# Two chained cross-attentions over 32 batches: the heads of the first scored twice, four at once, and the order of keys and first batches rewritten

## The chip, the cores and the metric

The kernel runs on one core of a Trainium2 chip. The metric is the time of one execution on the device in microseconds (us). A core has five engines with a queue each, executed in order: TensorE (PE, with its weight loads PEld), VectorE (DVE), ScalarE (ACT), GpSimd (POOL) and SyncE (SP), which here only issues DMAs. Products land in PSUM, eight banks of 2 KB per partition; everything else is computed in SBUF.

## The reference

Inputs are `x` and `ctx`, both 32 batches of 256 tokens by 256 columns, and the weights. L0 attends from x to ctx with 16 heads of 16 columns, but adds only batch 0's result, `att[0]`, to all batches. L1 is an attention of one head per batch, an MLP of four hidden units on its result, a second attention over that, and two scaled sums. All is float32.

```python
def _L0_xattn_ref(tgt, memory, Wq, Wk, Wv):
    q = (tgt @ Wq.T).reshape(B, N, NH, dk).transpose(0, 2, 1, 3)   # k, v from memory
    scores = jnp.einsum('bhqd,bhkd->bhqk', q, k) * scale
    probs = jax.nn.softmax(scores, axis=-1)
    att = jnp.einsum('bhqk,bhkd->bhqd', probs, v)
    tgt2 = att[0]                       # batch 0 alone, tokens by 256
    return tgt + tgt2
...
    norm_X = _layernorm(input_features, norm1_w, norm1_b)          # input_features: ctx
    norm_F_L = _layernorm(query_feature, norm2_w, norm2_b)         # query_feature: x after L0
    attended = _attention(norm_F_L, norm_X, norm_X, scale)
    h = jax.nn.gelu(attended @ fc1_w.T + fc1_b, approximate=False)
    cross_attended = h @ fc2_w.T + fc2_b
    norm_cross = _layernorm(cross_attended, norm3_w, norm3_b)
    self_attended = _attention(norm_cross, norm_cross, norm_cross, scale)
    skip_connect = cross_attended + gamma1 * self_attended
    return norm_F_L + gamma2 * skip_connect
```

## The kernel before

A batch is a tile of 128 partitions by 2 by 256: two tokens to a partition. All of x stays in SBUF (`x_all`); ctx comes in groups of four batches (`cq`, four buffers). The order of the instructions on each engine is the order of the program text: nothing is rescheduled (`manual_schedule`, line 69), and an instruction that waits holds up all behind it on its engine.

**Start (lines 100 to 153, 299 to 313).** SP loads batch 0 of x and ctx, small vectors, then ctx groups and x; ACT's queue loads the three weights. PE transposes x0, Wq, c0, Wk (`turned`, L179); four copies empty PSUM.

**Heads (L0).** `project(j)` (L316) makes q and k of heads 4j to 4j+3, each head on 32 partitions of its own. `head_scores(p)` (L376) scores two heads, queries on partitions; `exp_pair` (L348) takes the row maxima on DVE (L351) and the exponentials on ACT (L356); `head_turned` (L381) transposes the weights on PE and copies them by ACT and DVE (L388, L390); `head_values` multiplies by the values, `head_weighted` (L400) divides and writes a part of `att`. `head_step(s)` (L527) runs these in a pipeline over eight pairs of heads, and a list beside each step (lines 540 to 550) places the work for L1: `stats_c(n)` (DVE, the statistics of the keys of batch n, L188), `moments_c(q)` (POOL, mean and 1/deviation of four batches: eight small operations, L198 to L210, one of them a power, L203), `norm_c(n)` (POOL, two operations in place, L255), `turn_c(n)` (PE, four transposes, and a copy to `nxT`, L275), and the setups of the small matrices.

**Between.** `att` is added to batches 0 to 7 on DVE (L638) and to the others by DMAs that accumulate (L562). Batches 0 and 1, 2 and 3, 4 to 7 get moments on POOL (`moments_x`), `norm_x(n)` (one half on POOL, L262, the other on ACT, L264) and `turn_x(n)` (transposes, then `nfT` on ACT, L572).

**The loop over batches.** `first_step(s)` (from line 682) runs for s from 0 to 34. In step s, in this order: `cross_turned(s-2)` (transposes of weights, `pt_e`), statistics of x of batch s+8 and keys of batch s+12 (DVE), at every fourth step `moments_both` (POOL: keys and queries of four batches each), `turn_x(s+1)`, `norm_x(s+4)`, `turn_c(s+4)` from s = 4 on, `norm_c(s+8)`, the products with values at some steps, and `cross_scores(s)` (L590; maximum on DVE, L598; exponentials on ACT, L601). POOL also clears tiles in steps 8 to 17 (L711). Work of the MLP and of the second attention is put between and beside later steps (`third_a` to `third_d`, on POOL and DVE; `scale_skip` on POOL from step 25 on). A last part finishes the second attention and stores the output.

The line that ties norming and turning of keys to a step is, before:

```python
        if s + QB < B and s >= QB:
            turn_c(s + QB)
        if s + 2 * QB < B:
            norm_c(s + 2 * QB)
```

Of the kernel before, what the change touches and what calls it, by code (L numbers as in the profile page):

```python
# [15 lines left out]
P = 128  # L16
D = 256
# [10 lines left out]
def tile_xattn_seq(  # L28
# [49 lines left out]
    ps0 = l0_psum.enter_context(tc.tile_pool(name="ps0", bufs=2, space=PSUM))  # L78
# [26 lines left out]
    for name, w in (("q", wq), ("k", wk_w), ("v", wv)):  # L105
        w_nat[name] = wk.tile([P, NC, D], F32, tag="e", name=f"w{name}_nat", bufs=6)
        nc.scalar.dma_start(w_nat[name], w.rearrange("(c p) d -> p c d", p=P))
# [38 lines left out]

    ident = const.tile([P, P], F32)
# [12 lines left out]
    qT = l0.tile([P, NH // 4, D], F32)  # L160
    kT = l0.tile([P, NH // 4, D], F32)
# [28 lines left out]
    def moments(st, n, name):  # L190


# [5 lines left out]
        nc.gpsimd.tensor_sub(df, st[:, :, 1:2], st[:, :, 4:5])  # L198
        nc.gpsimd.tensor_add(sm, st[:, :, 1:3], st[:, :, 4:6])
        nc.gpsimd.tensor_mul(sq, df, df)  # L200
        nc.gpsimd.tensor_scalar(v4, sm[:, :, 1:2], 4.0 / D, 4 * EPS, ALU.mult, ALU.add)
        nc.gpsimd.tensor_add(ve, v4, sq)
# [6 lines left out]
        nc.gpsimd.tensor_scalar(nm, sm[:, :, 0:1], -0.5, 0.0, ALU.mult, ALU.add)  # L209
        nc.gpsimd.tensor_mul(nmr, nm, rs)  # L210
        return rs, nmr
# [31 lines left out]

    def moments_both(q):

        rn = moments(st_of[q].rearrange("p k b t c -> p (k b t) c"), 2 * TQ, f"b{q}")
        for b in range(QB):
            mc_of[(q + 1) * QB + b] = *rn, b * NC
            mx_of[q * QB + b] = *rn, TQ + b * NC
# [21 lines left out]
    def turn_c(n, copy=nc.vector.tensor_copy):  # L271
        q, b = n // QB, n % QB
        if b == 0:
            nxT_of[q] = wk.tile([P, QB, NC, D], F32, tag="nxT", name=f"nxT_{q}", bufs=2)
        copy(nxT_of[q][:, b], turned(cq_of[q][:, b], "tp", f"c_{n}"))  # L275
# [40 lines left out]
    def project(j):  # L316
# [11 lines left out]
        nc.vector.tensor_scalar_mul(qT[:, j, :], pp[:, 0, :], DK**-0.5)  # L328
        nc.scalar.copy(kT[:, j, :], pp[:, 1, :])

    def project_values():
        nc.vector.tensor_copy(wvT, turned(w_nat["v"], "tp", "wv"))
# [10 lines left out]
        for t in range(NC):  # L343
            nc.vector.tensor_copy(
                v1[:, t, :, 0:DK], pp[:, t, :].rearrange("p (h e) -> p h e", e=DK)
            )

    def exp_pair(sc, name):  # L348

        nm = small.tile([P, 2, NC], F32, tag="nm2", name=f"nm2_{name}")  # L350
        nc.vector.tensor_reduce(nm, sc, AX.X, ALU.max, negate=True)  # L351
        es = []
        for i in range(2):
            e = wk.tile([P, NC, D], F32, tag="e", name=f"e_{name}_{i}", bufs=6)
            for qt in range(NC):
                nc.scalar.activation(  # L356
                    e[:, qt, :], sc[:, i, qt, :], AF.Exp, bias=nm[:, i, qt : qt + 1]
                )
            es.append(e)
        return es  # L360
# [15 lines left out]
    def head_scores(p):  # L376
        sc = ps0.tile([P, 2, NC, D], F32, tag="s2", name=f"sc_h{p}")
        pair_products((p, qT[:, p // 2, :], kT[:, p // 2, :], [sc[:, i] for i in range(2)]))
        e_of[p] = exp_pair(sc, f"h{p}")

    def head_turned(p):  # L381
        if p % 2 == 0:
            eT_of[p // 2] = wk.tile([P, QB, NC, D], F32, tag="eTq", name=f"eT_h{p // 2}", bufs=2)
        for i, e in enumerate(e_of.pop(p)):
            dst = eT_of[p // 2][:, p % 2 * 2 + i]
            pe = turned(e, "et", f"eh_{p}_{i}")
            if i == 0:
                nc.scalar.copy(dst, pe)  # L388
            else:
                nc.vector.tensor_copy(dst, pe)  # L390
# [4 lines left out]
    def head_values(j):  # L395
        col_of[j] = by_columns(
            tp_bank, f"h{j}", lambda kt, i: v1[:, kt, 4 * j + i, :], eT_of.pop(j)
# [59 lines left out]
    def setup_m():  # L457
# [5 lines left out]
        nc.gpsimd.tensor_scalar(m5_nmean, m5_sum, -1.0 / D, 0.0, ALU.mult, ALU.add)  # L463
        nc.gpsimd.tensor_scalar(m5c, m5, m5_nmean, 0.0, ALU.add, ALU.add)
        nc.gpsimd.tensor_mul(k6[0:NM, :], m5c, w3r)
# [49 lines left out]
    def setup_output():  # L515
        nc.gpsimd.tensor_mul(w_h, m5, g2r)
        nc.gpsimd.tensor_mul(g1r, g1r, g2r)
        nc.gpsimd.tensor_mul(tail, tail, g1r)
        nc.gpsimd.tensor_add(w_h, w_h, tail)
        nc.gpsimd.tensor_add(w_h, w_h, bias2)  # L520
        nc.gpsimd.tensor_mul(g1r, g1r, k6[0:NM, :])
# [5 lines left out]
    def head_step(s, beside=()):  # L527
        if 0 <= s - 2 < NH // 2:
            head_turned(s - 2)
        if s < NH // 2:  # L530
            head_scores(s)
        if s % 2 == 1 and 0 <= s // 2 - 1 < NH // 4:
            head_values(s // 2 - 1)
        if s % 2 == 0 and 0 <= s // 2 - 2 < NH // 4:
            head_weighted(s // 2 - 2)
        for f, *args in beside:
            f(*args)

    project(0)
    head_step(0, [(project_values,), (stats_c, 0), (stats_c, 1)])  # L540
    head_step(1, [(project, 1), (stats_c, 2), (stats_c, 3), (moments_c, 0), (setup_fc1,)])
    head_step(2, [(stats_c, 4), (setup_queries,), (norm_c, 0), (norm_c, 1)])
    head_step(3, [(project, 2), (stats_c, 5), (norm_c, 2), (norm_c, 3), (setup_m,)])
    head_step(4, [(stats_c, 6), (turn_c, 0), (setup_outer,)])
    head_step(5, [(project, 3), (stats_c, 7), (moments_c, 1), (turn_c, 1)])
    head_step(6, [(stats_c, 8), (setup_gram,), (setup_output,), (norm_c, 4), (norm_c, 5)])
    head_step(7, [(stats_c, 9), (turn_c, 2), (norm_c, 6), (norm_c, 7)])
    head_step(8, [(turn_c, 3)])
    head_step(9, [(stats_c, 10)])
    head_step(10, [])  # L550
# [34 lines left out]
    def cross_scores(n):  # L585
# [11 lines left out]
        nm = small.tile([P, NC], F32, tag="nm", name=f"nm_{n}")  # L597
        nc.vector.tensor_reduce(nm, sc, AX.X, ALU.max, negate=True)  # L598
        e = wk.tile([P, NC, D], F32, tag="e", name=f"e_{n}", bufs=6)
        for qt in range(NC):  # L600
            nc.scalar.activation(e[:, qt, :], sc[:, qt, :], AF.Exp, bias=nm[:, qt : qt + 1])  # L601
        e_of[n] = e
# [31 lines left out]
    for q in range(2, 4):  # L634
        add_attention(q * QB, (q + 1) * QB)

    def add_and_stats(n):
        nc.vector.tensor_add(x_all[:, n], x_all[:, n], att)  # L638
        stats_x(n)

    add_and_stats(0)
    add_and_stats(1)
    moments_x(0, 0, 2)
    turn_c(4, nc.scalar.copy)
    turn_c(5, nc.scalar.copy)
    values(0)
    add_and_stats(2)
    add_and_stats(3)
    turn_c(6, nc.scalar.copy)
    turn_c(7, nc.scalar.copy)  # L650
    values_turned(0)
    norm_x(0)
    norm_x(1)
    moments_x(0, 2, 4)
    values(1)
    for n in range(4, 8):
        add_and_stats(n)
    turn_x(0)
    values_turned(1)
    norm_x(2)  # L660
    norm_x(3)
    stats_c(11)
    moments_x(1, 0, 4)
    moments_c(2)
# [424 lines left out]
```

## Time and profile before

| | us |
|---|---|
| three runs | 260.51, 264.87, 264.16 (median 264.16) |
| the profiled execution | 260.04, its span 258.3 |
| mean granted clock of TensorE | 0.967 |
| kT of the first heads ready | 11.18 |
| last part of `att` ready | 52.27 |
| scores of batch 0 start; of batch 8 end | 61.71; 95.42 |

The span is the time from the first to the last instruction of that execution; 1.74 us lie around it. In a line of the timeline the first number is the start and the second the duration in us, of as many instructions as the x at its end tells; then follow the engine, the line of the code, the operation, what it writes and reads, and in brackets the idle time of the engine before it, with what ended that. A slice of the page's second part is 6.46 us.

### The profile page before, as it was taken

The page shows a single profiled execution, that of the slowest core. Times are in us where ns is not written, and L with a number is a line of the kernel's source. Part 1 is how long each engine was busy: PE and PEld are TensorE (multiplying, and loading weights), DVE is VectorE, ACT ScalarE, POOL GpSimd, SP SyncE. Part 2 cuts the span into 40 slices and gives each one's busy share as a digit, 9 for nine tenths or more (in the row PEclk, how much of TensorE's full clock was granted, in tenths as well). Part 3 has the DMA queues.
Part 4 walks back from the last instruction along what each step waited for, and adds up shares of the span by engine and source line. Part 5 has one row for each costly group of instructions (what it writes and reads, how often), then busy time and mean ns, then how long its engine had stood idle before and what let it go on. Part 6 is the DMA issues. An engine that isn't in the chain of part 4 may idle for free.

```text
span 258.3 us, 4919 instructions
## 1 busy us (share of the span) xinstructions
PE 226.9 (88%) x1797; PEld 167.3 (65%) x1797; DVE 171.8 (67%) x371; ACT 144.4 (56%) x297; POOL 185.6 (72%) x298
## 2 busy tenths in 40 slices
PE   3878989977699999999999999989999699899960
PEld 3655666645487787978888796666666356565530
DVE  1369669799738587776868565465445567877482
ACT  1126454444686787677858984656743655454610
POOL 7006827989999989999958989992419808999200
PEclk9999999997979999999999999999999979999995
DMA  6859997059398766718000000000000024343466
GB/s 204 279 190 381 384 388 278 4 100 192 63 241 221 125 202 114 213 28 141 0 3 0 0 3 0 4 0 0 0 3 0 4 81 162 123 159 132 161 237 256
DMA packets 17526, 32.76 MB, mean 127 GB/s; under 512 B 1175, under 2 KB 2142, under 8 KB 17502
## 3 DMA queue, kind: packets, MB, share of 16 engines
q1 hardware_dynamic: 12462, 23.28, 24.8%
q0 software_dynamic: 3168, 6.29, 14.7%
q10 hardware_dynamic: 1872, 2.88, 3.1%
q8 instruction: 14, 0.23, 0.4%
q14 instruction: 10, 0.08, 0.1%
HBM read 17.73 MB, written 8.39 MB: 101 GB/s over the span
## 4 chain that ended last, share of the span: by engine, by line
PE 63%; POOL 15%; DVE 12%; ACT 3%; issue 3%; DMA 1%; DVEq 0%; ACTq 0%; POOLq 0%
PE sc L590 19%; PE sc L368 9%; PE pt_x L179 5%; PE pt_c L179 4%; PE pt_e L179 4%; PE pv L282 3%; PE pu L282 3%; PE po L368 3%; POOL rs_x L203 2%; POOL r L777 2%; PE pf L282 2%; PE pp L321 2%; POOL cq L255 2%; PE ph L282 2%; DVE x_all L934 1%
## 5 line engine op out<-in xcount | busy, mean ns | idle before, releaser
L590 PE MATMUL sc<-nxT,nfT 128*128 128x256 f32 x256 | 64.3, 396 | 0.3 <-ACT nfT L572 0.3
L590 PEld LDWEIGHTS sc<-nxT,nfT 128*128 128x128 f32 x256 | 47.9, 197 | 11.5 <-issue 4.9
L598 DVE TENSOR_REDUCE nm<-sc 128x2 f32<-128x512 f32 x32 | 22.1, 691 | 37.1 <-PE sc L590 20.7
L601 ACT ACTIVATE e<-sc,nm 128x256 f32<-128x256 f32 x64 | 26.8, 470 | 26.1 <-DVE nm L598 26.1
L581 POOL TENSOR_TENSOR x_all<-x_all,w_bc 128x512 f32<-128x512 f32 x32 | 39.6, 1275 | 0.0
L572 ACT ACTIVATE nfT<-pt_x,bq,wq 128x256 f32<-128x256 f32 x64 | 33.3, 582 | 0.0
L179 PE MATMUL pt_x<-ident,x_all 128*128 128x128 f32 x132 | 21.3, 287 | 8.4 <-DMA x_all<-in_x_dram 4.3
L255 POOL TENSOR_SCALAR cq<-cq,rs_b,nmr_b 128x256 f32<-128x256 f32 x40 | 24.8, 708 | 0.0
L188 DVE BATCH_NORM_STATS2 st<-x_all 128x6 f32<-128x256 f32 x64 | 23.9, 415 | 0.3
L179 PEld LDWEIGHTS pt_x<-ident,x_all 128*128 128x128 f32 x132 | 16.2, 147 | 9.4 <-POOL wkT L153 4.2
L179 PE MATMUL pt_e<-ident,e 128*128 128x128 f32 x128 | 20.0, 276 | 2.6 <-ACT e L601 2.5
L356 ACT ACTIVATE e_h<-sc_h,nm_h 128x256 f32<-128x256 f32 x32 | 12.6, 475 | 17.1 <-DVE nm_h L351 17.1
L179 PE MATMUL pt_c<-ident,cq 128*128 128x128 f32 x132 | 20.5, 280 | 1.6 <-DVE ut L801 0.8
L275 DVE COPY nxT<-pt_c 128x512 f32<-128x512 f32 x28 | 19.0, 677 | 4.1 <-PE pt_c L179 4.1
L368 PE MATMUL po<-w_out,vt 32*128 32x256 f32 x128 | 17.9, 412 | 3.4 <-DVE vt L808 2.2
L934 DVE TENSOR_TENSOR x_all<-po,x_all 128x512 f32<-128x512 f32 x26 | 16.7, 684 | 6.0 <-PE po L368 4.2
L188 DVE BATCH_NORM_STATS2 st<-cq 128x6 f32<-128x256 f32 x56 | 20.7, 411 | 0.0
L179 PEld LDWEIGHTS pt_e<-ident,e 128*128 128x128 f32 x128 | 15.4, 141 | 7.3 <-ACT e L601 3.9
L608 ACT COPY eTq<-pt_e 128x512 f32<-128x512 f32 x32 | 18.7, 587 | 1.9 <-PE pt_e L179 1.8
L368 PE MATMUL sc<-tt,ut 32*128 32x256 f32 x128 | 19.4, 403 | 0.0
L368 PE MATMUL sc<-ut 32*128 32x256 f32 x128 | 19.4, 413 | 0.0
L179 PEld LDWEIGHTS pt_c<-ident,cq 128*128 128x128 f32 x132 | 15.5, 143 | 3.6 <-DVE ut L801 1.0
(190 smaller groups left out, 464.9 us busy)
## 6 DMA issues: line engine op xcount, KB each, us to landing
out_dram<-x_all SPq DMA_DIRECT2D x16, 512.0 KB
x_all<-in_x_dram SPq DMA_DIRECT2D x6, 1024.0 KB
x_all<-att POOLq DMA_DIRECT2D x6, 1024.0 KB, 9.2
cq<-in_ctx_dram SPq DMA_DIRECT2D x5, 1024.0 KB
cq<-in_ctx_dram ACTq DMA_DIRECT2D x2, 1024.0 KB
x_all<-in_x_dram SPq DMA_DIRECT2D x1, 1792.0 KB
cq<-in_ctx_dram SPq DMA_DIRECT2D x1, 768.0 KB
wq_nat<-in_L_xattn_Wq_dram ACTq DMA_DIRECT2D x1, 256.0 KB
```

Source lines behind the costliest of these rows:

```text
L179: nc.tensor.transpose(pt[:, dc, t * P : (t + 1) * P], src[:, t, dc * P : (dc + 1) * P], ident)
L188: nc.vector.bn_stats(st[:, t, :], src[:, t, :])
L255: nc.gpsimd.tensor_scalar(row, row, rs[:, i + t, :], nmr[:, i + t, :], ALU.mult, ALU.add)
L275: copy(nxT_of[q][:, b], turned(cq_of[q][:, b], "tp", f"c_{n}"))
L282: nc.tensor.matmul(pg[SL * b : SL * (b + 1), 0, :], weights(kc, b), moving[:, b, kc, :], start=(kc == 0), stop=(kc == NC - 1),)
L368: nc.tensor.matmul(dst[i][:, t, :], lhs[r : r + SL, t * P : (t + 1) * P], rhs[r : r + SL, :], start=True, stop=True,)
L572: nc.scalar.activation(nfT_of[n][:, dc, :], px[:, dc, :], AF.Identity, bias=bq[:, dc : dc + 1], scale=wq2[:, dc : dc + 1],)
L581: nc.gpsimd.tensor_mul(x_all[:, n], x_all[:, n], w2_bc.unsqueeze(1).to_broadcast([P, NC, D]))
L590: nc.tensor.matmul(sc[:, qt, :], nfT[:, dc, qt * P : (qt + 1) * P], nxT[:, dc, :], start=(dc == 0), stop=(dc == NC - 1),)
L598: nc.vector.tensor_reduce(nm, sc, AX.X, ALU.max, negate=True)
L601: nc.scalar.activation(e[:, qt, :], sc[:, qt, :], AF.Exp, bias=nm[:, qt : qt + 1])
L934: nc.vector.tensor_add(x_all[:, n], po[i], x_all[:, n])
```

## The change

It does the following.

- Four matmuls of zeros open PE's queue.
- Four heads are scored at once, by `pair_products` with two pairs. `head_queries(j)` scores with the queries on the partitions and takes the negative row maxima into a column of `m_all`; `head_maxima(j)` transposes these and adds them to the queries' spare row (`qmT`), against a row of ones in kT (`k_ones`); `head_keys(j)` scores again with the keys on the partitions, so that the exponentials need no maximum and no transposes. `head_turned` and `exp_pair` are gone. qT and kT have two buffers in place of four.
- `head_step(j)` runs over four foursomes, with three places for other work in each. Keys of batches 0 to 11 get statistics and moments there and just behind, `norm_c` of 0 to 9 before, 10 and 11 among the first batches; in the loop `norm_c` runs for 12 to 15 in steps 1 to 3 and, from step 8 on, for s+8. `turn_c` runs for s+7 in steps 1 to 24; `nxT` has three buffers. `load_c` of groups 4 to 7 moves.
- x of batches 0 to 3 gets `att` added, statistics, moments and norm one batch at a time, of 4 to 7 two at a time, with the small operations of the moments on DVE and only the power on POOL; batches 4 to 7 get `att` by DMA.
- The small setups of `setup_m` and `setup_output` move from POOL to DVE, several copies from DVE to ACT.

The diff, cut:

```diff
-    ps0 = l0_psum.enter_context(tc.tile_pool(name="ps0", bufs=2, space=PSUM))
+    ps0 = l0_psum.enter_context(tc.tile_pool(name="ps0", bufs=1, space=PSUM))
...
+    zeros = l0.tile([P, D], F32)
+    nc.vector.memset(zeros, 0.0)
+    idle = bank("et", "p_idle")
+    for i in range(4):
+        nc.tensor.matmul(idle[:, i % NC, :], zeros[:, 0:P], zeros, start=True, stop=True)
...
-    qT = l0.tile([P, NH // 4, D], F32)
-    kT = l0.tile([P, NH // 4, D], F32)
+    qT = l0.tile([P, 2, D], F32)
+    kT = l0.tile([P, 2, D], F32)
+    qmT = l0.tile([P, 2, D], F32)
+    m_all = l0.tile([P, 2, NC, QB, SL], F32)
+    nc.gpsimd.memset(m_all, 0.0)
...
-    def moments(st, n, name):
+    def moments(st, n, name, eng=None):
+        eng = eng or nc.gpsimd
...
-        nc.gpsimd.tensor_sub(df, st[:, :, 1:2], st[:, :, 4:5])
+        eng.tensor_sub(df, st[:, :, 1:2], st[:, :, 4:5])
...
         nc.gpsimd.tensor_tensor(
             rs.rearrange("p n o -> p (n o)"),
...
+        def product():
+            eng.tensor_scalar(nm, sm[:, :, 0:1], -0.5, 0.0, ALU.mult, ALU.add)
+            eng.tensor_mul(nmr, nm, rs)
...
-        nc.vector.tensor_scalar_mul(qT[:, j, :], pp[:, 0, :], DK**-0.5)
-        nc.scalar.copy(kT[:, j, :], pp[:, 1, :])
+        nc.vector.tensor_scalar_mul(qT[:, j % 2, :], pp[:, 0, :], DK**-0.5)
+        nc.scalar.activation(kT[:, j % 2, :], pp[:, 1, :], AF.Identity, bias=k_ones)
...
+    def head_queries(j):
+        s0, b0 = head_bank("s0", f"sq_{2 * j}")
+        odd = [bank("et", f"sq_{2 * j + 1}_{i}") for i in range(2)]
+        qk = qT[:, j % 2, :], kT[:, j % 2, :]
+        pair_products((2 * j, *qk, b0), (2 * j + 1, *qk, odd))
+        for sc, b in ((s0, slice(0, 2)), (odd[0], 2), (odd[1], 3)):
+            m = m_all[:, j % 2, :, b, DK]
+            nc.vector.tensor_reduce(
...
+    def head_maxima(j):
+        pm = bank("tp", f"pm_{j}")
+        for t in range(NC):
+            nc.tensor.transpose(
...
+        nc.vector.tensor_add(qmT[:, j % 2, :], pm[:, 0, :], qT[:, j % 2, :])
+    def head_keys(j):
+        s1, b1 = head_bank("s1", f"sk_{2 * j}")
+        s0, b0 = head_bank("s0", f"sk_{2 * j + 1}")
+        kq = kT[:, j % 2, :], qmT[:, j % 2, :]
+        pair_products((2 * j, *kq, b1), (2 * j + 1, *kq, b0))
+        eT_of[j] = wk.tile([P, QB, NC, D], F32, tag="eTq", name=f"eT_h{j}", bufs=2)
+        nc.scalar.activation(eT_of[j][:, 2:4], s0, AF.Exp)
+        nc.scalar.activation(eT_of[j][:, 0:2], s1, AF.Exp)
...
+    head_step(
+        0,
+        [(project_values,), (project, 1), (stats_c, 0)],
+        [(setup_fc1,), (stats_c, 1)],
+        [(stats_c, 2), (stats_c, 3), (moments_c, 0), (setup_queries,)],
+    )
+    head_step(
+        1,
+        [(head_values, 0), (project, 2), (norm_c, 0), (norm_c, 1)],
+        [(head_weighted, 0), (stats_c, 4)],
+        [(stats_c, 5), (stats_c, 6), (norm_c, 2), (norm_c, 3)],
+    )
+    head_step(
+        2,
+        [(head_values, 1), (project, 3), (stats_c, 7), (moments_c, 1)],
+        [(head_weighted, 1), (turn_c, 0, on_scalar), (setup_m,)],
+        [
+            (turn_c, 1, on_scalar),
+            (turn_c, 2, on_scalar),
+            *((norm_c, n) for n in range(4, 8)),
+            (stats_c, 8),
+            (setup_outer,),
+        ],
+    )
+    head_step(
+        3,
+        [(head_values, 2), (turn_c, 3, on_scalar), (load_c, 4), (stats_c, 9)],
+        [(head_weighted, 2), (stats_c, 10)],
+        [(turn_c, 4, on_scalar), (stats_c, 11), (moments_c, 2), (turn_c, 5, on_scalar)],
+    )
+    head_values(3)
+    setup_gram()
+    setup_output()
+    turn_c(6, on_scalar)
+    load_c(5)
+    norm_c(8)
+    norm_c(9)
+    stats_c(12)
+    head_weighted(3)
...
+    def add_first(n, meanwhile):
         nc.vector.tensor_add(x_all[:, n], x_all[:, n], att)
         stats_x(n)
+        ends = first_moments(n, n + 1)
+        meanwhile()
+        ends()
+    add_attention(QB, 2 * QB)
+    turn_c(7, on_scalar)
     values(0)
+    load_c(6)
+    add_first(0, lambda: stats_c(13))
     values_turned(0)
+    values(1)
     norm_x(0)
+    norm_c(10)
+    add_attention(2 * QB, 3 * QB)
+    turn_x(0)
+    add_first(1, lambda: (stats_c(14), stats_c(15)))
+    values_turned(1)
     norm_x(1)
+    norm_c(11)
+    moments_c(3)
...
-        if s + QB < B and s >= QB:
-            turn_c(s + QB)
-        if s + 2 * QB < B:
+        if 0 < s < B - 2 * QB + 1:
+            turn_c(s + 2 * QB - 1)
+        if 0 < s < QB:
+            norm_c(s + 3 * QB - 1)
+            if s == QB - 1:
+                norm_c(s + 3 * QB)
+        elif 2 * QB <= s < B - 2 * QB:
             norm_c(s + 2 * QB)
...
+            softmax = cross_scores(s)
+            if s <= QB:
+                turn_x(s + 1)
+            if s < 2:
+                add_first(s + 2, softmax)
+                norm_x(s + 2)
+            else:
+                softmax()
...
-        w = late.tile([P, TG, n, n], F32, tag=f"w{n}", name=f"w_{name}", bufs=2)
+        w = late.tile([P, TG, n, n], F32, tag=f"w{n}", name=f"w_{name}", bufs=1)
...
-        21: [(third_a, 1), (third_b, 0)],
+        21: [(third_b, 0), (third_a, 1)],
```

## The prediction

> **What bounds the kernel now.** I read first the page's busy shares and its 40 slices, for the stretches in which TensorE (PE) isn't full.
>
> ```profile
> PE 226.9 (88%) x1797; PEld 167.3 (65%) x1797; DVE 171.8 (67%) x371; ACT 144.4 (56%) x297; POOL 185.6 (72%) x298
> ...
> PE   3878989977699999999999999989999699899960
> ...
> POOL 7006827989999989999958989992419808999200
> ```
>
> PE is full from the 12th slice (71 us) to the 26th (168 us); its gaps lie before 6 us, at 52 to 71 us and at the end. GpSimd (POOL) is as full as PE from 70 to 130 us. So two engines are near the bound in the loop over batches, and a schedule that ties one closely to the other is dangerous. The chain of waits, read next, agrees: from 86 to 149 us it is PE from one end to the other, 3.75 us a step, and at 50 to 70 us it goes through POOL's moments.
>
> The third view is the timeline at step 11 of the loop. `norm_c` normalizes a batch of keys on POOL, `turn_c` transposes it on PE (`pt_c`); batch 19 is normed at step 11.
>
> ```profile
> 104.20 0.69 DVE L598 TENSOR_REDUCE nm<-sc 128x2 f32<-128x512 f32 x1 [1.43 <-ACT x_all L264]
> 104.81 0.75 DVE L188 BATCH_NORM_STATS2 st<-x_all 128x6 f32<-128x256 f32 x2
> 105.47 0.74 DVE L188 BATCH_NORM_STATS2 st<-cq 128x6 f32<-128x256 f32 x2
> ...
> 106.29 0.23 POOL L198 TENSOR_TENSOR df_b<-st 128x16 f32<-128x16 f32 x1
> ...
> 107.58 2.94 POOL L203 TENSOR_TENSOR rs_b<-ve_b,neg_half 128x16 f32<-128x16 f32 x1
> ...
> 110.99 0.56 POOL L262 TENSOR_SCALAR x_all<-x_all,rs_b,nmr_b 128x256 f32<-128x256 f32 x1
> 111.53 1.09 POOL L255 TENSOR_SCALAR cq<-cq,rs_b,nmr_b 128x256 f32<-128x256 f32 x2
> ```
>
> The scores of batch 10 ended at 104.15. DVE takes their maximum, then the statistics (to 106.2); POOL's `moments_both` takes 106.29 to 110.99, 4.70 us, of which one power is 2.94; behind it stand `norm_x`(15) and `norm_c`(19), done at 112.62: 8.47 us after the scores of batch 10. PE's step 12:
>
> ```profile
> 107.20 0.60 PE L179 MATMUL pt_e<-ident,e 128*128 128x128 f32 x4
> 107.64 0.60 PE L179 MATMUL pt_x<-ident,x_all 128*128 128x128 f32 x4
> 108.08 0.60 PE L179 MATMUL pt_c<-ident,cq 128*128 128x128 f32 x4
> 108.51 1.89 PE L590 MATMUL sc<-nxT,nfT 128*128 128x256 f32 x8
> ```
>
> At 108.08 it turns keys, then scores. Today those are batch 16, normed long ago: turning runs 4 batches ahead of scoring and norming 8.
>
> **The change, part by part.**
>
> (a) Start. Four matmuls of zeros keep PE busy before x arrives at 4.26. Today PE's first transposes take 0.213 us each (0.85 for four), later ones 0.11, though the granted clock reads 1.00. If the zeros end that slow time, the landing of the key weights (SP's queue shows it at about 6.15) sets the pace: transposes 0.45, two copies 0.8, two products 0.9, qT 0.43, kT 0.38 make kT ready at 9.35, not 11.18: **-1.8** (from 0, where PE starts slow all the same, to -2.0).
>
> (b) Heads, from kT to the last `att`: today 11.18 to 52.27, 41.1 us. The change drops 64 transposes of weights (16 times 0.44 us of PE) and 16 copies of 0.6 to 0.68 on ACT and DVE, and scores twice. Eight matmuls on four row groups take 1.1 us (202.00 to 203.13, a later stage), as four on two do today. But the maxima now stand in a chain: scores 1.1, maxima 1.23 + 0.69 + 0.69 less overlap = 2.4 (rows L351, L598), qT and sum 0.42 each, scores again 1.1, first exponential 1.03 (L924), which frees the bank for the next four heads. Walked along the queues from kT, the scores of the four foursomes start at 0, 10.6, 17.7 and 27.5: the first carries the values' products, whose bank waits for a maximum, and project 1 (to 6.95); the third carries statistics (0.7), two key copies on ACT and `setup_outer`'s transposes. The fourth scores to 28.6; maxima 31.0; statistics and sum 32.1; keys 33.2; exponentials 35.25; a key copy 35.85; values and gram 37.7; six output rows now on DVE 2.2; statistics 0.7; `att` at 41.1. **0** (from -5 to +3). The saved work is PE's and ACT's; the chain is DVE's.
>
> The Trainium skill's TensorEngine Tiling (Array Packing), section "PSUM Bottleneck", speaks against the expected gain: packing speeds the products, not the emptying of PSUM. Here 1.1 us of products face 2.4 us of maxima. By packing alone the heads would be some 7 us shorter; by that rule they aren't.
>
> (c) From `att` to the end of the scores of batch 8: today 52.27 to 95.42, 43.1 us. After: add and two statistics 1.47, five small DVE operations 1.0 (0.2 each, from rd and att), the power of two columns 0.7 (1.65 for 8, 2.92 for 16, so 0.16 a column), the product 0.35, norm 0.6, transposes 0.5, half of nfT 0.6: scores of batch 0 start 5.4 after `att`, today 9.4. Then POOL's queue: batch 1's power stands behind `norm_c`(10) 1.1 and a DMA issue 1.4 (scores at +9.8), batch 2's behind `norm_c`(11) and `moments_c`(3), 4.4 together (+15.9); batch 3's nfT stands on ACT behind the norms of 4 and 5, which wait for DVE 2.4 and a power 1.3 (+23.5); batch 4 at +28.7 (today +26.0), batch 8 ends at +44.8. **+1.7** (-5 to +4).
>
> (d) The loop. Turning now runs 7 batches ahead of scoring, norming still 8 from step 8 on: the lead falls from four steps to one. At step 12 `pt_c` turns batch 19, whose norm ends 8.47 us after the scores of batch 10, while PE arrives 3.93 after them. All that follows in PE's queue, scores 12 included, waits 4.4 us (transposes after the wait 0.35). Statistics come only after the maximum of the scores before, so POOL can't catch up: the next round is as late again. A round of four steps costs 8.8 + 1.73 + 4.23 + 4.45 = 19.2 us, not 14.94. The five places: batch 16 at step 9, 3.5 (its norm ends at 100.04 today, `pt_c` stands at 96.13); 19, 4.4, and 0.6 for 20 behind a memset and a DMA issue; 23, 4.4 (127.6 against 123.06); 27, 4.4 (142.6 against 138.05); 29 behind `third_a`, which waits for the gelu, 0.8; 31 at step 24, behind `third_c` and `moments_x` on POOL, 7.3 (today 160.64 against 153.16). **+25.4**. Below: if rows before were POOL's own backlog only, the largest lateness is paid once, 7.5; above, each place a microsecond worse, 31.
>
> (e) Clock. Where PE stood 3.3 us (56.3 to 59.7), the granted clock was 0.66 in 60 to 65 us and the scores took 2.91, not 1.99; after 2.3 us, 3.21. The five gaps of 3.5 to 7.3 us are longer: 1.0 each, **+5** (0 to +10). TensorE: Matmul & The Clock Gate, "HAM oscillation", warns of idle gaps over 3.4 us, with 3.4 us at half clock after: half of that, 1.7 a gap, would be 8.5 as an estimate.
>
> (f) End of the loop: steps 25 to 27 have no `turn_c` (three times 0.44), the waits of 0.94 (161.9) and 0.4 of the 0.78 at 169.4 go: **-2.7** (-5 to 0). The end, 200 us on, is untouched.
>
> The moments and rows moved from POOL to DVE, some 10 us, free POOL before step 8 only, where it then waits for statistics anyway; batches 4 to 7 added by one more DMA (9.2 us to landing) have 15 us until they are read. SP's queue issues the loads of keys 4 to 7 earlier, around the eight stores of `w_out` (0.66 to 0.80 each), and the first is read some 30 us later; the two issues of 0.38 that stood on ACT go. The cleared maxima (0.52, a memset of 128x512) lie before 6 us beside PE's transposes; were they late, kT is still 4 us off. Key copies moved from DVE to ACT take 0.59 for 0.68 and are counted where they stand in a chain. Fewer buffers for `e` (three live at a time) and `w` cost nothing: `third_a`(1) now stands behind its reader.
>
> Sum: -1.8 + 0 + 1.7 + 25.4 + 5 - 2.7 = **+27.6** on the profiled execution's own 260.04 us (span 258.3): **287.6**. That execution is the fastest of those shown; the median is 264.16, so the median after may lie 1 to 2% above. Below 2% a measurement of this kernel tells nothing from no change.
>
> **Rivals.** *The stalls come, the rest is kinder*: clock not lost and heads or first batches 5 to 8 us shorter, 260.04 - 1.8 - 5 + 25.4 - 2.7 = 276; for it, the heads do lose 7 us of PE work. Chance 0.28. *Only a backlog* (the other side): if POOL, freed of 10 us, holds its norms ahead, `pt_c` never waits; the loop stays at 15 us a round and the change brings 260.04 - 1.8 - 4 - 2.7 = 251 to 253. It decides at one point: `norm_c`(19) must end within 3.9 us of the scores of batch 10, not 8.5. Against it, 4.70 of moments alone are more than that. Chance 0.07. *Backlog paid once*: 260.04 - 1.8 + 7.5 - 2.7 = 263, within 2%; it needs statistics that don't wait for PE's progress, and DVE's order says they do. Chance 0.03. *Worse*: a second wait in the rounds, or cold products throughout, over 297: 0.07. The forecast, 279 to 297: 0.55. Four heads at once not running at once would add 4 us to it, no case of its own.
>
> The range leaves out 251 to 263 and the worst: **271 to 297**. Slower by over 2%: 0.90; within 0.03; faster 0.07.
>
> **What would show it.** Right: in the page's slices PE has holes at steps 9, 12, 16, 20 and 24, PE's idle before `pt_c` released by POOL cq (L255 today, some 20 us in all), POOL idle before `df_b` released by DVE statistics, rounds of 19 us between the scores of batches 10, 14 and 18. (a): kT near 9.4; (b) `att` near 50.5. Wrong: rounds of 15 us, or `pt_c` released by nothing. What would upset it most is a power shorter than 2.9 us, or statistics ahead of the maximum.

## The result, and the profile after

| | before | after |
|---|---|---|
| runs, us | 260.51, 264.87, 264.16, 263.94 (median 264.05) | 295.98, 296.07, 296.15, 297.75 (median 296.11) |
| profiled execution; its span | 260.04; 258.3 | 295.98; 293.8 |
| mean granted clock | 0.967 | 0.910 |

The changed kernel takes 1.128 times as long (95% interval 1.116 to 1.140). The forecast was 287.6 us with 271 to 297. Executions of one kernel differ with the granted clock, mostly by some 5 us (the kernel before from 259 to 265 us in all, `lead6` below 269.5 and 274.3 to 274.6) and once by 17 (`l4_both`), and a profile shows one of them (`lead4`, `filled`, `l4_project` and `l4_rows` the longest, `lead6` the shortest), so terms are read from stretches of the profiles and not from times alone. The two profiles of the table, cut at the places that the forecast's terms use (kT ready, last part of `att`, end of the scores of batch 8, start of those of batch 24, end; the loop from start to start of the scores), account for all 35.5 us of the spans, to a tenth:

| stretch | before | after | difference | forecast |
|---|---|---|---|---|
| to kT | 11.18 | 9.71 | -1.5 | -1.8 (a) |
| kT to `att` | 41.1 | 46.9 | +5.8 | 0 (b) |
| `att` to the end of scores 8 | 43.2 | 44.9 | +1.7 | +1.7 (c) |
| scores 8 to scores 24 | 60.1 | 91.6 | +31.5 | +30.4 (d, e) |
| scores 24 to the end | 104.7 | 102.6 | -2.1 | -2.7 (f) |

The page of the changed kernel: shares, then the 40 slices of 7.3 us.

```profile
PE 236.2 (80%) x1813; PEld 171.2 (58%) x1813; DVE 171.7 (58%) x409; ACT 141.6 (48%) x276; POOL 180.2 (61%) x281
...
PE   8688777667599969498598599199999969899980
...
POOL 7006594689786693983913747939550970999600
PEclk9879998959979999799689799689999986999996
```

PE does some 9 us more of busy time and POOL 5 less; no engine is nearer its bound. Where the kernel before had a full row of nines from the 12th slice on, there are holes now in the slices from 103, 118, 140, 162 and 184 us, and in POOL's row other holes beside them: the two engines take turns to wait. In the slices of all these holes but the first the PEclk digit falls to 6 or 7.

The timeline of the changed kernel at step 11, DVE, POOL and PE in turn, answers to the one that the prediction read in the kernel before.

```profile
113.72 0.69 DVE L676 TENSOR_REDUCE nm<-sc 128x2 f32<-128x512 f32 x1 [1.43 <-ACT x_all L295]
114.99 0.74 DVE L202 BATCH_NORM_STATS2 st<-x_all 128x6 f32<-128x256 f32 x2
...
115.81 0.23 POOL L213 TENSOR_TENSOR df_b<-st 128x16 f32<-128x16 f32 x1 [4.37 <-DVE st L202]
117.11 2.94 POOL L218 TENSOR_TENSOR rs_b<-ve_b,neg_half 128x16 f32<-128x16 f32 x1
120.52 0.56 POOL L293 TENSOR_SCALAR x_all<-x_all,rs_b,nmr_b 128x256 f32<-128x256 f32 x1
121.06 1.10 POOL L286 TENSOR_SCALAR cq<-cq,rs_b,nmr_b 128x256 f32<-128x256 f32 x2
...
117.16 0.60 PE L193 MATMUL pt_x<-ident,x_all 128*128 128x128 f32 x4
121.68 1.44 PE L193 MATMUL pt_c<-ident,cq 128*128 128x128 f32 x4 [3.92 <-POOL cq L286]
```

The scores of batch 10 ended at 113.62, the norm of batch 19 ends at 122.16: 8.5 us, as the walk from the old trace had it (8.47). PE stands in front of `pt_c` for 3.92 us, and POOL had itself stood for 4.37 us before the moments, waiting for DVE's statistics, which stand on DVE behind the maximum of PE's scores. That is a ring: PE, DVE, POOL, PE. The transposes after the wait take 1.44 us for 0.60, so PE also comes out of it slow.

### The profile page after: what moved, and what is told of

It reads as the page before. It is cut to its first block, busy times and chain, and to the rows that moved or that the text cites. A ratio compares the mean times of both kernels' runs of the same rounds, so it can differ in the third digit from the quotient of the medians.

```text
span 293.8 us, 4957 instructions
## 1 busy us (share of the span) xinstructions
PE 236.2 (80%) x1813; PEld 171.2 (58%) x1813; DVE 171.7 (58%) x409; ACT 141.6 (48%) x276; POOL 180.2 (61%) x281
## 4 chain that ended last, share of the span: by engine, by line
PE 60%; POOL 19%; DVE 10%; ACT 4%; issue 3%; DVEq 0%; ACTq 0%; POOLq 0%
PE sc L666 17%; PE sc L385 8%; PE pt_c L193 4%; POOL rs_b L218 4%; PE pt_e L193 3%; PE pt_x L193 3%; POOL cq L286 3%; PE pp L352 3%; PE po L385 3%; PE pv L313 3%; PE pu L313 3%; POOL r L870 2%; POOL rs_x L218 2%; PE pf L313 2%; PE ph L313 2%
## 5 line engine op out<-in xcount | busy, mean ns | idle before, releaser
L666 PE MATMUL sc<-nxT,nfT 128*128 128x256 f32 x256 | 70.5, 424 | 0.8 <-ACT nfT L648 0.8
L666 PEld LDWEIGHTS sc<-nxT,nfT 128*128 128x128 f32 x256 | 51.0, 211 | 14.2 <-issue 4.5
L193 PE MATMUL pt_c<-ident,cq 128*128 128x128 f32 x132 | 23.5, 299 | 25.3 <-POOL cq L286 22.4
L193 PEld LDWEIGHTS pt_c<-ident,cq 128*128 128x128 f32 x132 | 15.9, 149 | 30.6 <-POOL cq L286 26.3
L306 DVE COPY nxT<-pt_c 128x512 f32<-128x512 f32 x24 | 16.3, 680 | 24.3 <-PE pt_c L193 24.3
L193 PEld LDWEIGHTS pt_x<-ident,x_all 128*128 128x128 f32 x132 | 17.2, 153 | 9.4 <-POOL x_all L293 7.8
L385 PE MATMUL po<-w_out,vt 32*128 32x256 f32 x128 | 19.1, 433 | 3.4 <-DVE vt L901 2.2
L1027 DVE TENSOR_TENSOR x_all<-po,x_all 128x512 f32<-128x512 f32 x26 | 16.7, 684 | 7.2 <-PE po L385 5.0
L385 PE MATMUL sc<-tt,ut 32*128 32x256 f32 x128 | 20.3, 418 | 0.0
L286 POOL TENSOR_SCALAR cq<-cq,rs_b,nmr_b 128x256 f32<-128x256 f32 x32 | 19.6, 691 | 0.0
L286 POOL TENSOR_SCALAR cq<-cq,rs_c,nmr_c 128x256 f32<-128x256 f32 x32 | 18.7, 614 | 0.2
L193 PEld LDWEIGHTS pt_e<-ident,e 128*128 128x128 f32 x128 | 16.3, 147 | 3.4 <-issue 1.4
```

Of the source, the lines that this page charges most:

```text
L193: nc.tensor.transpose(pt[:, dc, t * P : (t + 1) * P], src[:, t, dc * P : (dc + 1) * P], ident)
L286: nc.gpsimd.tensor_scalar(row, row, rs[:, i + t, :], nmr[:, i + t, :], ALU.mult, ALU.add)
L385: nc.tensor.matmul(dst[i][:, t, :], lhs[r : r + SL, t * P : (t + 1) * P], rhs[r : r + SL, :], start=True, stop=True,)
L666: nc.tensor.matmul(sc[:, qt, :], nfT[:, dc, qt * P : (qt + 1) * P], nxT[:, dc, :], start=(dc == 0), stop=(dc == NC - 1),)
```

## The experiments

All times are medians; the kernel before ran beside each group of them, on the same chip as the group, at 259.2 to 259.9 us. A range in brackets behind a ratio is its 95% interval.

### The lead of the turn, undone and by itself

`lead4` is the changed kernel with one line as before; `lead6` puts the turn one step later than the change does; `before_lead7` is the kernel before with the new lead alone (with the buffers that it needs, and `third_a`(1) behind `third_b`(0) as in the change).

```diff
 lead4
-        if 0 < s < B - 2 * QB + 1:
-            turn_c(s + 2 * QB - 1)
+        if QB <= s < B - QB:
+            turn_c(s + QB)
 lead6
+        if 2 <= s < B - 6:
+            turn_c(s + 6)
 before_lead7 (from the kernel before)
-        if s + QB < B and s >= QB:
-            turn_c(s + QB)
+        if 0 < s < B - 2 * QB + 1:
+            turn_c(s + 2 * QB - 1)
```

> The changed kernel with one edit: keys are turned 4 batches ahead of scoring again (steps 4 to 27 turn s+4), all else as changed. Theory (the lead makes the stalls): the waits before pt_c for POOL's norms go (22.4 us of idle in the changed kernel's profile), and with them the cold products behind them; between the scores of batches 8 and 24 the changed kernel took 91.6 us, the kernel before 60.1, so 31.5 us go. Steps 25 to 27 get a turn back (+1.3), steps 1 to 3 lose one (-1.3), and the 2.1 us that the end of the loop had won go: 296.1 - 31.5 + 2.1 = 267 us (262 to 271), rounds of four steps 15 us. Rival 1 (POOL and DVE have become too slow in the loop whatever the lead; for instance the three nxT buffers or the key loads hold it up): still over 285, with PE waiting at other places. Rival 2 (the heads and first batches cost most of the 32 us): no better than 285 either, with the loss ahead of step 8.

> The changed kernel with the turn 6 batches ahead in place of 7 (steps 2 to 25 turn s+6). Theory (a norm that is 7.9 to 8.5 us late by the scores' clock meets a PE that now comes one step of 3.7 us later): the waits of 3.9 us fall to 0 to 0.8, that at the end from 6.9 to about 2.4, and little cold clock: the loss is a threshold, not a slope; 264.5 + 5 = 269 us, range 265 to 274. Rival (each step of lead costs its third of the 31.5 us): about 285.

> The kernel before with the turn of keys 7 batches ahead alone (steps 1 to 24 turn s+7), and what makes room for the third nxT buffer, as in the change: four buffers for e, one for w, third_b(0) ahead of third_a(1). Heads, first batches and norms as before. Theory (the lead alone is enough for the loss): the loop from step 8 to 24 gets the changed kernel's 31.5 us, the end of the loop gives 2.1 back, and since moments_both stands in steps 3 and 7 of this kernel too, steps 4 and 8 add up to 5 us each: 264 + 29.4 + 0 to 10 = 293 to 304, middle 299 us. Rival (the lead hurts only with the change's other parts, such as its norms that start later): 264 to 270.

| | time, us | ratio to before | scores 8 to 24 | idle before `pt_c` by POOL |
|---|---|---|---|---|
| before | 259.2 | | 60.06 | 0 |
| after | 296.1 (beside a before of 264.05) | 1.128 | 91.60 | 22.4 |
| lead6 | 274.4 (profiled 269.5) | | 64.52 | 7.3 |
| lead4 | 264.5 | 1.019 (1.012 to 1.025) | 60.07 | 0 |
| before_lead7 | 306.0 | 1.184 (1.174 to 1.193) | 89.49 | 35.6 in all |

The slices of PE in lead4 (first line) have no hole from the 13th to the 25th; the group of `pt_c` on PE (second line; the last column is the idle time before it and who ended it) no longer waits for POOL.

```profile
PE   8688786747649999999999999889999879899970
...
L193 PE MATMUL pt_c<-ident,cq 128*128 128x128 f32 x132 | 20.0, 276 | 1.5 <-DVE ut L894 0.8
```

The same group in the changed kernel:

```profile
L193 PE MATMUL pt_c<-ident,cq 128*128 128x128 f32 x132 | 23.5, 299 | 25.3 <-POOL cq L286 22.4
```

With the lead back, the loop takes what it took before to a hundredth of a microsecond: the whole 31.5 us belongs to this line, and nothing else of the change (three `nxT` buffers, key loads at other times, norms that start later) costs anything between batches 8 and 24. The converse holds too: put into the old kernel alone, the lead brings 29.4 us there, and 18 more before batch 8. That is above the range that I gave, since I had counted up to 5 us each for steps 4 and 8 (4.0 and 3.9 of wait came) and nothing for step 1, where `pt_c` stands 8.9 us while POOL makes two sets of moments:

```profile
74.82 1.42 PE L179 MATMUL pt_c<-ident,cq 128*128 128x128 f32 x4 [8.91 <-POOL cq L255]
```

The loss is no slope. From the scores of batch 8 to those of batch 31 the kernel before takes 101.0 us, the changed one 129.7, lead6 108.1: one batch of lead less takes three quarters of the loss away, not a third, because PE then comes a whole step (3.7 us) later to a norm that was 3.9 us late. The waits of the rounds shrink from 3.92 to 0.88; that for batch 31 stays at 3.83, for 2.4 expected, and the median of 274.4 lies just above the range of 265 to 274.

### What makes the norm late: the moments ahead of it

```diff
 norm_first
-        if b == QB - 1 and 3 <= q + 2 < NQ:
-            if q + 3 < NQ:
-                moments_both(q + 2)
-            else:
-                moments_x(q + 2, 0, QB)
...
         elif 2 * QB <= s < B - 2 * QB:
             norm_c(s + 2 * QB)
+        if b == QB - 1 and 3 <= q + 2 < NQ:
+            (the same lines)
```

> The changed kernel with one edit: in every step the moments (moments_both, moments_x) are issued on POOL behind norm_x and norm_c, not ahead of them; the turn stays 7 batches ahead. Theory (what delays the last batch of a group is the 4.7 us of moments, which wait for the statistics, ahead of its norm): the waits of 3.9 us at steps 12, 16, 20 and of 6.9 at step 24 go, but the first batch of the next group, normed in the next step from these moments, now is the one that is late: by the forecast's walk its norm ends 2.1 + 4.7 + 0.56 + 1.09 = 8.5 us after the scores that started the statistics (up to 10.8 with a memset and a DMA issue between), and PE reaches its turn 7.7 after them: 0.8 to 3 us a round. So about a fifth to a half of the loop's 31.5 us stays: 296.1 - 31.5 + 7 (to 15) = 272 us, range 267 to 281. Rival (the rounds are set by POOL's total work or by DVE, not by the order): over 288, rounds still 20 us or more.

Measured: 280.9 us, 1.085 (1.082 to 1.087); scores 8 to 24 76.8 us; waits 11.6 us. The wait of step 12 is gone and one of step 13 is there, as the timeline of PE shows:

```profile
119.05 1.89 PE L666 MATMUL sc<-nxT,nfT 128*128 128x256 f32 x8
121.22 0.60 PE L193 MATMUL pt_x<-ident,x_all 128*128 128x128 f32 x4
124.89 0.33 PE L193 MATMUL pt_c<-ident,cq 128*128 128x128 f32 x1 [3.07 <-POOL cq L286]
```

It is the next group's first batch that comes late now, behind a memset (0.95) and a DMA issue (1.32) on POOL; in the later rounds, where only a memset of 0.2 or none of this is left, the wait is 1.0. So the order on POOL matters, by half of the loss, and the mechanism is the one named. My middle value was too kind (272; the 281 measured is the edge of the range): it had 7 us left of the loop's loss, and the waits alone are 11.6, since those of 2.3 at step 9 and 3.6 at step 24 weren't in it; the slower turns and products behind the waits make it 16.7.

### The clock behind the gaps

Idle places of PE are filled with matmuls whose results the following transposes overwrite.

```diff
 filled
     def turned(src, tag, name, fill=0, moving=None):
         pt = bank(tag, f"pt_{name}")
+        for i in range(fill):
+            nc.tensor.matmul(pt[:, i % NC, :], ident, moving, start=True, stop=True)
...
-            turn_c(s + 2 * QB - 1)
+            turn_c(s + 2 * QB - 1, fill={9: 6, 12: 8, 16: 8, 20: 8, 24: 14}.get(s, 0))
...
+        gap = bank("tp", "p_gap")
+        for i in range(4):
+            nc.tensor.matmul(gap[:, i % NC, :], zeros[:, 0:P], zeros, start=True, stop=True)
         pp = bank("et", "pp_v")
```

> The changed kernel with matmuls put into PE's idle times, whose results are overwritten: 4 before the values' products (idle 2.07 us), 9 before the first transposes of x (4.2), 6, 8, 8, 8, 14 before the turn of keys in steps 9, 12, 16, 20, 24 (2.8, 3.9, 3.9, 3.9, 6.9), 0.43 us each, so that they should end inside the wait. Theory (idle time lets the clock fall, and the slow products behind it are a cost of their own): behind the gaps the turns take 0.6 not 1.4 us, the scores of 12, 16, 20, 24 1.9 not 2.8 to 3.6, those of batch 0 1.9 not 3.8, the values' products 2.0 not 3.75, with the same waits for POOL; loop 6 to 9 us shorter, first scores 2 to 3, first foursome 3: 296.1 - 12 = 284 us, range 280 to 290. Rival (the clock falls for another reason, or the rounds are POOL's and DVE's, so that warm products only wait longer): the same as the changed kernel, 294 to 299, the idle before pt_c growing by what the products save.

Measured: 285.6 us, 1.100 (1.092 to 1.109). PE's timeline in its step 12, and the clock's digits of its page:

```profile
117.23 3.62 PE L192 MATMUL pt_c<-w_out,ident 128*128 128x256 f32 x16
121.30 0.33 PE L195 MATMUL pt_c<-ident,cq 128*128 128x128 f32 x1 [0.45 <-POOL cq L288]
```
```profile
PEclk9997988799799999999999999999999997999995
```

The norm is as late as ever, but PE works through the wait and leaves it at full clock: scores of batch 12 1.9 us, not 2.82, those of 16 and 20 1.9, not 3.6. The loop from 8 to 24 falls from 91.6 to 86.2 us: 5.4 us of the loss are the clock's, 26.1 the wait's. In the heads it was different. The first foursome took 10.7 us (13.65 unfilled), as the theory wants, though in `lead6` it took 10.7 without any filling; and the second took 9.0, not 7.6, with a granted clock of 0.66 from 20 to 25 us, and kT to `att` gained only 1.2 in all (this execution is 7.7 us shorter than the changed kernel's, the median 10.5). Three other places of low clock (0.66 to 0.67 from 20 to 25, 40 to 45 and 50 to 55 us) had taken the place of the one filled. In the first batches the warm scores of batch 0 (2.0 for 3.78) bought nothing: batch 2 starts at 72.5 for 72.7, and the transposes of its x wait for the norm on POOL in both (2.5 and 1.5 us).

### The heads: two terms of the 5.8 us

These start from lead4, so that the loop doesn't cover them.

```diff
 l4_project
-        [(project_values,), (project, 1), (stats_c, 0)],
+        [(project, 1), (project_values,), (stats_c, 0)],
 l4_rows
-        nc.vector.tensor_mul(w_h, m5, g2r)          (and the five others)
+        nc.gpsimd.tensor_mul(w_h, m5, g2r)
...
             (setup_outer,),
+            (setup_output,),
...
     setup_gram()
-    setup_output()
 l4_no_zeros
-    for i in range(4):
-        nc.tensor.matmul(idle[:, i % NC, :], zeros[:, 0:P], zeros, start=True, stop=True)
```

> lead4 (the changed kernel with the turn 4 batches ahead) with project(1) ahead of the values' products, which wait for a PSUM bank that the maxima empty. Theory (in the first foursome PE stands 1.7 to 2.1 us there, and what follows runs at a lowered clock): PE goes on with project(1) at once, the idle falls under 1 us, the values' products take 2.0 us, and the scores of the second foursome start 8.6 us after those of the first, not 12.3 (lead4) or 13.7 (changed kernel). All later foursomes and att follow: att 3.6 us earlier, about 53.1 not 56.7; 264.5 - 3.6 = 261 us, range 259 to 263. Rival (the foursomes behind it are bound by something that doesn't follow, such as loads of keys or POOL): second foursome earlier, att no earlier than 55.5, time as lead4.

> lead4 with setup_output's six rows on POOL again, behind setup_outer in the third foursome's step, where POOL is idle (45.7 to 48.6 us). Theory (the six rows, 3.1 to 3.3 us on DVE between the gram and the last part of att, stand in the chain): att at 53.7, not 56.7; first scores 3 us earlier; 264.5 - 3 = 261.5 us, range 260 to 263. Rival (something else releases att then, such as PE's transposes of the last foursome): att no earlier than 55.5, time as lead4.

> lead4 without the four matmuls of zeros. Theory (they end PE's slow first transposes): kT at 11.2 us as in the kernel before, not 9.7 to 10.1; the transposes of x0, Wq, c0, Wk 0.85 us each; time 1.3 us longer, 265.8 (264.5 to 267). Rival (the start is set by the loads): kT within 0.3 us of lead4's, same time.

**l4_project**: 260.8 us, 1.005 (1.003 to 1.008). First foursome 8.2 us, `att` at 52.51. PE in the changed kernel, from the first scores on:

```profile
9.77 1.15 PE L385 MATMUL sq<-kT,qT 32*128 32x256 f32 x16 [0.59 <-ACT kT L360]
12.98 3.75 PE L369 MATMUL pp_v<-wvT,c0T 128*128 128x256 f32 x8 [2.07 <-DVE m_all L405]
16.53 1.91 PE L352 MATMUL pp<-x0T,wqT 128*128 128x256 f32 x4
```

and in l4_project:

```profile
9.51 1.15 PE L385 MATMUL sq<-kT,qT 32*128 32x256 f32 x16 [0.59 <-ACT kT L360]
10.58 1.13 PE L352 MATMUL pp<-x0T,wqT 128*128 128x256 f32 x4
11.55 1.03 PE L352 MATMUL pp<-c0T,wkT 128*128 128x256 f32 x4
12.73 1.96 PE L369 MATMUL pp_v<-wvT,c0T 128*128 128x256 f32 x8
```

The wait for the bank is covered, and the values' products take half as long. All later foursomes moved with it.

But the slow products are not a fixed price of that wait. `lead6` has the code of the changed kernel up to the loop, and the same wait, and there they ran at full speed:

```profile
12.59 1.97 PE L369 MATMUL pp_v<-wvT,c0T 128*128 128x256 f32 x8 [2.07 <-DVE m_all L405]
```

Its first foursome took 10.7 us, and kT to `att` 44.3. In the five other profiles with this order and this wait (changed kernel, lead4, norm_first, l4_rows, l4_no_zeros) the products took 3.35 to 3.75 us and the foursome 12.1 to 13.7. So the 10.7 of `filled` doesn't show by itself that the filling helped in the heads. The new order does: in all three profiles that have it (l4_project, l4_both, recut) the foursome took 8.2 us.

**l4_rows**: 263.9 us, 1.015 (1.007 to 1.023). `att` at 53.48 (lead4 56.70), right to 0.2. The six rows stood there on DVE, 3.1 to 3.4 us in one stretch; in the changed kernel the first and last two of them are

```profile
52.17 0.65 DVE L561 TENSOR_TENSOR w_h<-m,g2r 5x256 f32<-5x256 f32 x1
...
54.53 0.67 DVE L565 TENSOR_TENSOR w_h<-w_h,bias 5x256 f32<-5x256 f32 x1
55.12 0.41 DVE L566 TENSOR_TENSOR g1r<-g1r,k 5x256 f32<-5x256 f32 x1
```

The scores of batch 0 came 2.3 us earlier, those of batch 8 2.9, but the median only 0.6, which leaves it above the range of 260 to 263: the single times overlap (261.2 to 264.3 here, 262.7 to 267.0 in lead4), so the time alone can't show this term. The profiles do: from DVE's copy of the gram (L545) to the end of `att` it takes 4.4 us in lead4 and 1.4 here.

**l4_no_zeros**: 264.9 us, 1.022 (1.017 to 1.026), and kT at 9.96, not at the 11.2 that I expected. This theory fell, and the rival's numbers came: kT within 0.2 us of lead4's, the time within 0.5. Without the zeros PE's first transposes start when x lands, at 3.90; with them at 4.64 to 4.75, behind the zeros, which take 3.6 to 3.8 us from 1.18 on. In l4_no_zeros:

```profile
3.90 1.09 PE L186 MATMUL pt_x<-ident,x_all 128*128 128x128 f32 x4 [3.90 <-DMA x_all<-in_x_dram]
4.79 1.06 PE L186 MATMUL pt_wq<-ident,wq_nat 128*128 128x128 f32 x4
7.09 1.03 PE L345 MATMUL pp<-x0T,wqT 128*128 128x256 f32 x4
```

kT lies between 9.32 and 10.60 in the nine kernels with zeros, and at 9.76, 9.96 and 11.18 in the three without (the second profile of the old start, in before_lead7, has 9.76). What differed in the profile of before was that x landed 0.4 to 0.5 later and the first products took 1.74 us, not 1.03.

### A version that beats both

```diff
 recut (on l4_project and l4_rows together, called l4_both)
-            (turn_c, 1, on_scalar),
-            (turn_c, 2, on_scalar),
+            (setup_outer,),
+            (turn_c, 1, on_scalar),
...
     setup_gram()
-    turn_c(6, on_scalar)
-    norm_c(8)
-    norm_c(9)
-    stats_c(12)
     head_weighted(3)
+    for n in range(4, 7):
+        turn_c(n, on_scalar)
...
-        if 0 < s < QB:
-            norm_c(s + 3 * QB - 1)
...
+        if 0 < s < B - 2 * QB:
             norm_c(s + 2 * QB)
...
+            if s in (2, 3):
+                stats_c(s + 3 * QB)
+            if s == 3:
+                moments_c(3)
```

> lead4 with both edits of the heads: project(1) ahead of the values' products, and setup_output's rows on POOL behind setup_outer. Theory (the two stand in one chain to att and add up): att at 49.5 us (52.5 with project(1) alone, less the 3 us of the rows), scores of batch 8 end near 95; POOL's rows push norm_c(8) and norm_c(9) behind att, which gives up to 0.9 back; 260.8 - 2.2 = 258.6 us, range 257 to 260.5: level with the kernel before (259.6). Rival (the first batches are bound by POOL's queue, whatever att does): 260 to 262.

> l4_both, and what else stands in the chains of waits before step 8 is moved: keys 1 to 7 are turned behind the products that wait for no ACT copy (setup_outer and head_values(3) no longer stand behind nxT copies; batches 4 to 7 after the last part of att), norm_c of 8 to 15 runs in the step before its old place in the kernel before (steps 0 to 7), statistics of 12 to 15 and moments_c(3) follow behind batches 0 to 3, values(1) behind the first transposes of x. Theory (the heads' remaining waits are 1.6 us twice, and the first batches' steps of 4 to 7 us are long because POOL and DVE do work there that isn't needed yet): att near 47 us, scores of batch 8 end near 91 (95.4 in the kernel before), 253 us, range 250 to 257. Rival (POOL is the bound in steps 4 to 8 then, with twelve norms and two sets of moments more): att near 47, but waits for POOL before pt_c or pt_x in steps 4 to 10 and no better than 257.

**l4_both**: 259.5 us, 0.9995 (0.996 to 1.003), `att` at 49.31: the two terms add up, and the kernel is level with the one before. **recut**: 255.7 us, 0.985 (0.982 to 0.987): faster than before by 1.5% (255.6 to 256.2 in six executions, where the lowest of the kernel before is 258.9), though that is under the 2% below which the prediction trusted no difference, and less than the 253 expected. `att` is at 47.00 as expected; the scores of batch 8 end at 91.9 for the 91 expected. Its page:

```profile
PE 222.4 (88%) x1813; PEld 162.9 (64%) x1813; DVE 167.5 (66%) x403; ACT 141.3 (56%) x276; POOL 183.0 (72%) x287
...
PE   8988685988499799999999998989999689899970
```

PE is busy 14 us less than in the changed kernel, and the one deep hole before the end (the 11th slice, 63 to 70 us) is the scores of batch 3, which wait 3.1 us for `nfT`. From kT to `att` it takes 36.4 us, where the kernel before takes 41.1 and the changed one 46.9. So the heads scored twice pay with this order around them and with the old lead. Whether the old heads would gain as much from such an order wasn't tested.

## Why the prediction was right or wrong

The direction, the cause in the loop and the places there were right; the size was 8 us short, and 5.8 of these were missing in the heads. The other terms came within 1.1 us each.

**(d) and (e), the loop: right.** 30.4 forecast, 31.5 measured, at the five steps named (9, 12, 16, 20, 24; waits of 2.8, 3.9, 3.9, 3.9, 6.9, with 0.4 at batch 29 for the small ones). The rounds from the scores of batch 10 on took 20.8, 22.3 and 22.3 us, where the walk had 19.2 and 1.0 for the clock. lead4 shows that the lead is the whole cause, norm_first that the moments ahead of the norm are what it meets, filled that 5.4 us of it are the clock. The forecast's 5 for that was right, though shared out differently: behind the three waits of 3.9 the scores lose 0.9, 1.7 and 1.7 us and the turns up to 0.8. By the starts of the scores filling gave back 0.6 us at step 12, 2.8 at step 16, 1.7 at step 20, 0.3 before the scores of batch 24 and nothing at step 9, for 1.0 a gap. The two waits that the term was taken from are 2.83 and 1.90 us by their rows, not 3.3 and 2.3; the scores of 3.21 us stand behind the second.

```profile
59.66 0.66 PE L179 MATMUL pt_x<-ident,x_all 128*128 128x128 f32 x4 [2.83 <-POOL x_all L262]
...
69.79 0.91 PE L179 MATMUL pt_e<-ident,e 128*128 128x128 f32 x4 [1.90 <-ACT e L601]
70.53 1.01 PE L179 MATMUL pt_x<-ident,x_all 128*128 128x128 f32 x4
71.33 3.21 PE L590 MATMUL sc<-nxT,nfT 128*128 128x256 f32 x8
```

The prediction's estimate of 8.5 named the Trainium skill's page TensorE: Matmul & The Clock Gate (section "HAM oscillation") and was too high. That section itself counts about 1.67 us of throttled time a gap, half of it lost; for five gaps that is 4.2 as an estimate, nearer to the 5.4 measured. Its warning of gaps over 3.4 us doesn't cover the waits of 1.90 and 2.07 us here that were followed by slow products.

**(c), first batches: right**, +1.7 both, and each batch came within 1.4 us: scores 0 to 4 start 6.1, 11.2, 16.1, 23.0 and 27.9 after `att`, for 5.4, 9.8, 15.9, 23.5 and 28.7 forecast. The first come later and the last earlier than forecast, so that the sum agrees to a tenth is partly luck.

**(b), heads: the term that failed.** "kT to `att` 0" came out as +5.8. By foursomes, from the start of one's scores to the next: 13.65, 7.6, 10.5 and 15.1 to `att`, where the walk had 10.6, 7.1, 9.8 and 13.6. Half is the first one: I saw the wait of the values' products for their bank, but costed all products at full clock, and behind that wait of 2.07 us they ran at 0.60 to 0.71 of it. The clock term had been set for the loop's gaps alone, though the rows that it was taken from showed slow scores behind a wait of 1.90. With that gap filled the foursome took 10.7, nearly the walk's 10.6; so it did in lead6, unfilled, where the clock stayed up. The clock is thus what the term left out, and when it falls stays open. Another 1.1 is the six rows: 3.36 us for 2.2. The other 1.6 is spread over the second to the fourth, with a granted clock of 0.79 and 0.87 between 40 and 50 us. The bound that I gave, +3 at the worst, was too narrow for a path on which PE stops in each foursome. The stretch itself varies between profiles of the same code: the new heads take 44.3 (lead6) to 47.0 (norm_first), the old ones 41.1 (before) and 42.8 (before_lead7), so the loss is 1.5 to 5.9 us and 5.8 lies near its upper end.

**(a), start: right in size by luck, wrong in cause.** The 1.5 us are there, but l4_no_zeros has 1.2 of them without the zeros. The term compared one profile with a walk, and one profile of an old start can be 1.4 us slow by itself.

**(f), end of the loop: right**, -2.1 for -2.7; lead4 gives it back (40.92 from scores 24 to 31, as before, where the changed kernel has 38.05).

**The rivals.** "Only a backlog" was to be decided by whether the norm of batch 19 ends within 3.9 us of the scores of batch 10; it ended 8.5 after them, in each round again, so "backlog paid once" falls too. "The rest is kinder" falls by (b), which went the other way. The rule of the Trainium skill's page TensorEngine Tiling (Array Packing), section "PSUM Bottleneck", agrees with the trace: 1.1 to 1.2 us of scores were followed by 2.42 us of maxima in every foursome, and the heads got no shorter. From the changed kernel to recut the packing is the same; what takes 10.5 us off the heads there is the order of the work around them, the rows' move to POOL and the clock behind fewer waits.

## What to carry to other kernels

A look-ahead has a latest producer: before an operation is moved earlier, walk back from it to the last thing it waits for, and if that is work which itself waits for the same engine's recent output, the lead has a threshold beyond which every round pays. One step less of lead may then be worth most of the loss, as here three quarters. When costing such a chain, allow for slow products behind every wait on the way, in the set-up as well as in the loop (here they came behind the same wait of 2.07 us in five profiles of six), and don't credit a gain to an edit from two profiles where repeats of the old start already differ by that much.

## What the runs showed of the hardware

- **A short idle time can halve the clock, and need not.** In the changed kernel 2.07 us of idle were followed by products of 3.75 us, at a granted clock of 0.60 from 15 to 20 us; in lead6 the same wait was followed by the same products in 1.97, at 1.00. In lead4 1.14 us before the third foursome (first line below) were followed by scores of 1.97 us and values of 1.88 for 1.07; in the changed kernel the same wait (second line) was followed by nothing of the kind. With one gap in the heads filled the low clock stood at other places there; in the loop, where PE is otherwise full, filling kept it at full speed (PEclk digits of 9 from the 12th to the 33rd slice). What decides it wasn't found.
- **Warming PE with zeros bought nothing at the start.** Four such matmuls took 3.6 to 3.8 us. The transposes behind them took 0.60 us for four in lead6 and up to 1.06 in l4_rows and filled, with the same code up to there; in l4_no_zeros they took 1.06 to 1.09, the last four 0.76, but started 0.7 to 0.9 us earlier.

```profile
30.00 1.97 PE L385 MATMUL sq<-kT,qT 32*128 32x256 f32 x16 [1.14 <-ACT eT_h L430]
31.00 1.15 PE L385 MATMUL sq<-kT,qT 32*128 32x256 f32 x16 [1.14 <-ACT eT_h L430]
```
